# Attention masks turned by DMA transposes instead of TensorE and ScalarE, in a two-layer graph network kernel

## The chip, the cores and the metric

The kernel runs on one core of a Trainium2 chip. The metric is the device time of one execution in microseconds (us). The kernel before takes 4320.45 us, the median of three runs (4317.54 to 4321.28).

## The reference

For each of 16 batches there are 1024 nodes with 256 features (`x`) and an adjacency matrix of 1024 x 1024 int32 (`adj`, about 3% ones). Two layers follow each other, and both use the same adjacency as a mask:

```python
def heads(x):
    return x.reshape(w, n, H, DH).transpose(0, 2, 1, 3)          # 8 heads of 32
q, k, v = heads(features @ Wq), heads(features @ Wk), heads(features @ Wv)
e = jnp.einsum('whqd,whkd->whqk', q, k)
e = jnp.where(e >= 0, e, ALPHA * e)                              # leaky relu, 0.2
attn = jax.nn.softmax(jnp.where(adj[:, None] > 0, e, NEG), axis=-1)
h = jnp.einsum('whqk,whkd->whqd', attn, v)
out = _layernorm(h, g1, b1)
out = jnp.concatenate([out, features], axis=-1) @ Wffn.T
x = _layernorm(out, g2, b2) + features
# second layer: two graph attentions, then a feed-forward net
def _gat(h, adj, W, a, out_features):
    Wh = h @ W
    e = leaky_relu(Wh @ a[:F] + swap(Wh @ a[F:]))                # 1024 x 1024 by broadcast
    return softmax(where(adj > 0, e, NEG), axis=1) @ Wh
h = _layernorm(x + _gat(_gat(x, W1, a1), W2, a2))
out = _layernorm(h + relu(h @ w_ff1 + b_ff1) @ w_ff2 + b_ff2)
```

Inputs and outputs are float32.

## The kernel before, in words

`unshifted_path` does the work with softmaxes that subtract no maximum; `general_path` is a second program that runs only if a check of sums and scores at the end asks for it, which it does not for these inputs.

Per batch and head, scores are made with keys on the partitions and queries along the row: for each of 8 key tiles t, two matmuls of 128x512 (L615) make a 128x1024 tile in PSUM. ScalarE scales it by 0.2 (L631), VectorE takes the maximum with the original (L633), ScalarE takes the exponential (L636), GpSimd multiplies it with the mask (L640), and TensorE multiplies the result with the values and with a column of minus ones for the sums, 32 columns of weights at a time (L655, `product`). These value products are called narrow below. VectorE also adds two pairs of tiles per head first (L699). After a head, VectorE turns the result (L716) and GpSimd divides by the sums (L723). When all heads of a batch are done, `rest(b)` runs: `rows_pair` (L792, L795, L812, L824) closes layer one, `attention`/`attend` (L860 to L885) with the products L915 and L940 are the two graph attentions, `hidden` and `feed_forward` (L980, L1008) the feed-forward net. `rest(b)` runs while the heads of batch b + 1 run.

Because keys lie on the partitions, the mask is needed with rows and columns exchanged. `mask_part(b, t, halves)` makes it for 128 queries: it loads 128x512 int32 of the adjacency into a buffer of the pool `pair` (L424 by the SP queue for batch 0, L420 by the ACT queue afterwards, two halves in one part), VectorE turns it into bytes, -1 or 0 in fp8, in a buffer `adjb` (L429), TensorE transposes these as pairs of bytes, that is as 2-byte elements, four transposes of 128x128 per part of two halves, into a PSUM buffer of the pool `misc` (L439), and ScalarE copies the PSUM buffer to the mask (L443). `mask_of(b, t)` reads one tile of it with a stride of two bytes. A mask is 1024 bytes x 8 on each partition, and there are two, so the mask of batch b + 1 is made during batch b. The multiply L640 of batch b waits for the parts of all queries; the graph attentions read the same mask (L880).

The queries and keys of a batch are split into a high and a low float32 part and stored to DRAM (L504, SP's queue), and read back for each head as stacks (`qs`, `ks`, four loads on SP's queue, L581); there are two buffers of each. The first layer's result of a batch is stored and fetched again too (L754, L761), and the output stored (L1023), all on SP's queue.

The order of all instructions on every engine is written out by a planner, `Order`, when the program is built. The parts above are generators that say which engine they need for how long (`on(PE=310)`), which buffers they take and give, and for what they wait. Each has a due time, its aim, as a share of the batch's planned time SLOT; the tables AIM (batches from the third on) and EARLY (batch 0 and 1) hold these shares. Whichever operation can start within 300 ns of the earliest and has the smallest aim goes next. A DMA is `load(n)`: 500 ns of its queue for each n, and a landing some 3.5 us later. The engines and queues then run these orders as they are, each instruction waiting by semaphores for what it needs; DMAs of both queues share eight semaphores, and a DMA waits until the earlier one on its semaphore has landed.

Of the kernel before, what the change touches and what calls it, by code (L numbers as in the profile page):

```python
# [11 lines left out]
BF = mybir.dt.bfloat16  # L12
F8 = mybir.dt.float8e4
I32 = mybir.dt.int32
AF = mybir.ActivationFunctionType
OP = mybir.AluOpType
# [4 lines left out]
P = 128  # L21
HALF = 512
# [164 lines left out]
def on(shared=False, delay=0.0, mode=None, **costs):  # L187
    return "on", (costs, shared, delay, mode)


def pause(time):
    return "pause", time


def wait(event):
    return "wait", event


def fire(event):
    return "fire", event  # L200


def take(pool):
    return "take", pool


def give(pool):
    return "give", pool


def start(thread, aim):
    return "start", (thread, aim)
# [21 lines left out]
def unshifted_path(  # L234
# [8 lines left out]
    nc = tc.nc  # L243
    B, N, D = x.shape
    NT = N // P
    NP = NT // 2
# [8 lines left out]
    QN = N // 4  # L255
# [4 lines left out]
    YW = D + 2  # L260
    NSUM = NT * H + 2 * NT
    NSCORE = 4 * NT
    SLOT = 253e3
    PACE = SLOT / (H * NT // 2)


    AIM = dict(mask0=0.602, x=1.454, x_step=-0.0104, mask=0.9396, mask_step=-0.0101, qk0=0.4907, qk1=1.7441,
               qk_step=-0.0518, v0=0.7416, v1=0.621, v_step=0.0547, rows=-0.079, rows_step=-0.0113, first0=0.2137,
               first1=-0.446, graph0=-0.0793, graph1=0.316, graph_step=0.0481, second=0.7493, second_step=-0.015,
               normed=1.0223, normed_step=-0.0115, ff_wait=(None, 0, 1, 0), ff=(0.5532, 0.1074, 3.6996, 1.0353),  # L270
               ff_step=0.0063, fast0=0.2312, fast1=0.6979, fast15=1.0127, lead=14.8372)

    EARLY = dict(x=2.6481, x_step=-0.1001, mask=0.5019, mask_step=0.0795, qk0=0.7532, qk1=1.2626, qk_step=-0.1325,
                 v0=0.2134, v1=1.5023, v_step=-0.0416, rows=-2.7213, rows_step=-0.3343, first0=-0.8482,
                 first1=-4.695, graph0=0.0441, graph1=-0.9035, graph_step=-0.1073, second=0.463,
                 second_step=0.0554, normed=0.7744, normed_step=0.0342, ff_wait=(None, 0, 1, 0),
                 ff=(2.0875, 0.7055, 1.5112, 0.6358), ff_step=0.0607)

    const = ctx.enter_context(tc.tile_pool(name="const", bufs=1))
    sb = ctx.enter_context(tc.tile_pool(name="sb", bufs=1))  # L280
    small = ctx.enter_context(tc.tile_pool(name="small", bufs=6))
    psum = ctx.enter_context(tc.tile_pool(name="psum", bufs=2, space=bass.MemoryType.PSUM))
    dram = ctx.enter_context(tc.tile_pool(name="dram", bufs=3, space=bass.MemoryType.DRAM))
    bufs = dict(misc=3, scores=2, acc=1, p=6, stacks=2, stage=2, adj=2, adjb=2, pair=18,
                xT=2, v=2, mask=2, hn=1, w8=2, big=1, job=1)
    work = Order(**bufs)

    def share(b, name):
        return (EARLY if b < 2 else AIM)[name]

    def misc(dtype=FT):
        return psum.tile([P, HALF], dtype, tag=f"misc{work.slot['misc']}", name="ps_m", bufs=1)

    def buf(shape, tag, name, dtype=FT):
        return sb.tile(shape, dtype, tag=tag, name=name, bufs=bufs[tag])


    ident = const.tile([P, P], FT, name="ident")
    make_identity(nc, ident)
    ident_b = const.tile([P, P], BF, name="ident_b")  # L300
    nc.vector.tensor_copy(ident_b, ident)
    eps = const.tile([P, 1], FT, name="eps")
    nc.gpsimd.memset(eps, EPS)
    minus_ones = const.tile([P, DH], FT, name="minus_ones")
# [18 lines left out]
    k = {}  # L323
# [15 lines left out]
    def load(n=1, latency=3500):  # L339

        return on(SP=500 * n, delay=latency)
# [56 lines left out]
    masks = {}  # L398
# [3 lines left out]
    stacks = {}  # L402

    def mask_part(b, t, halves):

        n = len(halves)
        ints = []
        if b:
            yield take("adj")
        elif halves[0]:  # L410
            yield wait(("mask", b, t, 0))
        for kh in halves:
            yield take("pair")
            ai = buf([P, HALF], "pair", "adj_i", I32)
            ints.append(ai)
            part = adj[b].rearrange("(u p i) k -> u i p k", p=P, i=2)[t // 2, t % 2, :, kh * HALF:(kh + 1) * HALF]
            if b:
                yield pause(1500)
                yield on(ACT=400, delay=3500)
                nc.scalar.dma_start(ai, part)  # L420
            else:
                yield pause(2000)
                yield load()
                nc.sync.dma_start(ai, part)  # L424
        yield take("adjb")
        ab = buf([P, 2 * HALF], "adjb", "adj_b", F8)
        for i, ai in enumerate(ints):
            yield on(DVE=336, shared=True)
            nc.vector.tensor_scalar(ab[:, i * HALF:(i + 1) * HALF], ai, 0.0, -1.0,  # L429
                                    op0=OP.is_gt, op1=OP.mult, saturate=False)  # L430
            yield give("pair")
        if b:
            yield give("adj")
        yield take("misc")
        pt = misc(BF)
        pairs = ab.bitcast(BF)
        yield on(PE=30 + 140 * n)
        for i in range(2 * n):
            nc.tensor.transpose(pt[:, i * P:(i + 1) * P], pairs[:, i * P:(i + 1) * P], ident_b)  # L439
        yield give("adjb")  # L440
        yield on(ACT=46 + 218 * n)
        k0 = 2 * halves[0]
        nc.scalar.copy(masks[b].bitcast(BF).rearrange("p (k q) -> p k q", k=NP)[:, k0:k0 + 2 * n, t * P:(t + 1) * P],  # L443
                       pt[:, :2 * n * P].rearrange("p (k q) -> p k q", k=2 * n))
        yield give("misc")
        for kh in halves:
            yield fire(("mask", b, t, kh))

    def make_mask(b, t0):
        yield take("mask")  # L450
        masks[b] = buf([P, NT * N], "mask", "mask", F8)
        parts = [(t, (kh,)) for kh in range(NH) for t in range(NT)] if b == 0 else [(t, (0, 1)) for t in range(NT)]
        for n, (t, halves) in enumerate(parts):
            yield start(mask_part(b, t, halves),
                        t0 + ((share(b - 1, "mask") if b else AIM["mask0"]) + share(b - 1, "mask_step") * n) * SLOT)

# [54 lines left out]
    def project_qk(b, g, t0):  # L511
        scratch[b, g] = dram.tile([2, P, 2, N], FT, name="qk_halves")
        for o in range(2):
            for nh in range(NH):
                yield start(qk_part(b, g, o, nh), t0 + (2 * o + nh) * share(b - 1, "qk_step") * SLOT)

# [20 lines left out]
    def project_v(b, g, t0):  # L537
        yield take("v")
        vs[b, g] = buf([P, NT, G * DH], "v", "v")
        for u in range(NP):  # L540
            yield start(v_part(b, g, u), t0 + share(b - 1, "v_step") * u * SLOT)

# [6 lines left out]
    def project(b, t0):  # L549
        yield take("xT")  # L550
        xTs[b] = buf([P, DC, N], "xT", "xT")
        for u in range(NP):
            yield start(x_pair(b, u), t0 + (share(b - 1, "x") + share(b - 1, "x_step") * u if b else 0.0) * SLOT)
        yield start(make_mask(b, t0), t0 + (0.5 if b else 0.0) * SLOT)
        for g in range(H // G):
# [35 lines left out]
    def pace(b):  # L591
        return PACE * {0: AIM["fast0"], 1: AIM["fast1"], B - 1: AIM["fast15"]}.get(b, 1.0)

    def all_scores():
        for b in range(B):
# [4 lines left out]
            for h in range(H):  # L600
                yield wait(("stack", b, h))
                q, kk = stacks[b, h]
                for t in range(NT):
                    due = t0 + (h * NT + t) / 2 * pace(b)
                    if b == 0 or t % 2 == 0:
                        yield aim(due, AIM["lead"] * PACE)
                        for _ in range(2 if b else 1):
# [877 lines left out]
```

## Time and profile before

The profile is of one execution of the kernel before.

| | |
|---|---|
| median of three runs | 4320.45 us |
| the profiled execution | 4317.81 us |
| its span, first to last instruction | 4315.9 us |
| mean granted TensorE clock | 0.990 |
| L439, transposes of the mask, PE | 512, 219 ns median, 52.2 us busy |
| L443, copies of the mask, ACT | 136 (120 of 582 ns, 16 of 376 ns) |
| L429, conversions, DVE | 256, 761 ns mean, 421 ns median in a steady batch |
| L640, multiply with the mask, POOL | 1024, 2431 ns |
| DMA, both queues | 344.79 MB, 80 GB/s mean |

Times are in microseconds unless marked ns. PE is TensorE, PEld its weight loads, DVE VectorE, ACT ScalarE, POOL GpSimd, SP the sync engine that only issues DMAs; SPq and ACTq are the issue of DMAs. L439 is line 439 of the kernel. "busy" is the union of an engine's instructions; matmuls overlap, so a mean duration of one is longer than the time it holds the queue. A row of waits names the waiting instruction, then the one whose end released it, then total us, times and the longest. A line of the order of time begins with start and length in us.

### The profile page before, as it was taken

How to read it: one execution, taken by the hardware profiler on the slowest of the kernel's cores; microseconds unless marked ns; L12 is line 12 of the kernel's file. 1: busy time of each engine (PE TensorE's matmuls, PEld its weight loads, DVE VectorE, ACT ScalarE, POOL GpSimd, SP SyncE). 2: the span in 40 equal slices, each digit the busy share in tenths (PEclk: the TensorE clock that was granted, in tenths of full speed). 3: DMA queues.
4: the chain of work that ended last, by engine and by line, in shares of the span. 5: the costliest groups of instructions: out<-in, count | busy, mean ns of one | idle time of the engine just before them, and what ended most of it. 6: DMA issues, size and time to landing. Idle time of an engine off the chain costs nothing.

```text
span 4315.9 us, 76274 instructions
## 1 busy us (share of the span) xinstructions
PE 4189.7 (97%) x30027; PEld 3030.3 (70%) x30027; DVE 3544.8 (82%) x5491; ACT 2942.7 (68%) x4362; POOL 2571.6 (60%) x1161
## 2 busy tenths in 40 slices
PE   8788999999999999999999999999999999999999
PEld 4466677677777777777777777777777777777687
DVE  6878878888888887879879788887889879788853
ACT  6756677777767677776776767677776776767632
POOL 5846467664757656574664757646575674747700
PEclk9999999999999999999999999999999999999999
DMA  6413223322232322323232222322323222222100
GB/s 188 125 54 99 69 76 87 91 72 86 74 94 67 96 84 68 90 71 89 84 84 81 79 81 79 91 73 81 91 74 89 81 84 84 74 79 57 30 20 21
DMA packets 156282, 344.79 MB, mean 80 GB/s; under 512 B 21750, under 2 KB 24332, under 8 KB 155916
## 3 DMA queue, kind: packets, MB, share of 16 engines
q1 hardware_dynamic: 112140, 260.13, 21.0%
q10 hardware_dynamic: 43776, 79.71, 6.6%
q8 instruction: 239, 3.92, 0.4%
q14 instruction: 127, 1.04, 0.1%
HBM read 239.09 MB, written 100.66 MB: 79 GB/s over the span
## 4 chain that ended last, share of the span: by engine, by line
PE 82%; DVE 11%; ACT 3%; POOL 1%; DMA 1%; issue 1%; SPq 0%; ACTq 0%; POOLq 0%; DVEq 0%
PE ps_a L655 17%; PE ps_s L615 11%; PE ps_m L915 10%; PE ps_m L980 9%; PE ps_m L940 9%; PE ps_m L1008 7%; PE ps_m L492 4%; DVE p L633 3%; PE ps_m L792 3%; PE ps_m L824 3%; PE ps_m L795 3%; PE ps_m L524 2%; PE ps_m L372 2%; DVE p L699 2%; POOL p L640 1%; DVE att L880 1%
## 5 line engine op out<-in xcount | busy, mean ns | idle before, releaser
L640 POOL TENSOR_TENSOR p<-p,mask 128x1024 f32<-128x1024 f32 x1024 | 2471.1, 2431 | 1425.5 <-ACT p L636 1044.1
L633 DVE TENSOR_TENSOR p<-p,ps_s 128x1024 f32<-128x1024 f32 x1024 | 1211.3, 1213 | 251.2 <-ACT p L631 248.1
L636 ACT ACTIVATE p<-p 128x1024 f32<-128x1024 f32 x1024 | 1082.2, 1059 | 302.3 <-DVE p L633 276.7
L631 ACT ACTIVATE p<-ps_s 128x1024 f32<-128x1024 f32 x1006 | 986.3, 1021 | 345.2 <-PE ps_s L615 283.0
L615 PE MATMUL ps_s<-qs,ks 128*128 128x512 f32 x2048 | 658.7, 437 | 30.6 <-DVE p L633 27.0
L655 PE MATMUL ps_a<-p,v 128*32 128x256 f32 x8192 | 561.9, 388 | 24.4 <-POOL p L640 24.3
L615 PEld LDWEIGHTS ps_s<-qs,ks 128*128 128x128 f32 x2048 | 352.6, 190 | 266.1 <-issue 114.8
L940 PE MATMUL ps_m<-y,att 128*128 128x256 f32 x2048 | 481.1, 382 | 12.6 <-ACT y L885 11.1
L915 PE MATMUL ps_m<-y,att 128*128 128x258 f32 x2048 | 477.1, 383 | 14.4 <-ACT y L885 12.9
L980 PE MATMUL ps_m<-rT,wf 128*128 128x256 f32 x2048 | 474.3, 383 | 9.4 <-ACT hid L989 4.3
L1008 PE MATMUL ps_m<-wf,hid 128*128 128x256 f32 x2048 | 475.7, 381 | 0.6 <-DVE hid L986 0.6
L915 PEld LDWEIGHTS ps_m<-y,att 128*128 128x128 f32 x2048 | 385.5, 190 | 89.3 <-ACT y L885 13.8
L980 PEld LDWEIGHTS ps_m<-rT,wf 128*128 128x128 f32 x2048 | 381.0, 190 | 85.9 <-issue 14.3
L699 DVE TENSOR_TENSOR p<-p 128x1024 f32<-128x1024 f32 x256 | 410.5, 1604 | 23.6 <-PE ps_a L655 23.4
L940 PEld LDWEIGHTS ps_m<-y,att 128*128 128x128 f32 x2048 | 378.4, 190 | 71.1 <-ACT y L885 11.3
L1008 PEld LDWEIGHTS ps_m<-wf,hid 128*128 128x128 f32 x2048 | 379.1, 190 | 63.6 <-issue 8.2
L655 PEld LDWEIGHTS ps_a<-p,v 128*32 128x32 f32 x8192 | 209.5, 109 | 289.3 <-issue 130.8
L655 PE MATMUL ps_a<-p,minus_ones 128*32 128x256 f32 x6144 | 405.8, 382 | 1.2 <-DVE p L699 1.2
L877 DVE SCALAR_TENSOR_TENSOR att<-first,second 128x1024 f32<-128x1024 f32 x256 | 359.7, 1405 | 32.4 <-ACT first L864 28.3
L880 DVE SCALAR_TENSOR_TENSOR att<-mask,att 128x1024 f32<-128x1024 fp8e4 x256 | 339.5, 1326 | 5.6
L655 PEld LDWEIGHTS ps_a<-p,minus_ones 128*32 128x32 f32 x6144 | 199.1, 111 | 138.3 <-issue 7.9
L885 ACT ACTIVATE y<-y,check 128x258 f32<-128x258 f32 x256 | 131.1, 512 | 220.4 <-DVE check L883 217.9
(101 smaller groups left out, 4330.0 us busy)
## 6 DMA issues: line engine op xcount, KB each, us to landing
qs<-qk_halves SPq DMA_DIRECT2D x256, 256.0 KB, 4.0
ks<-qk_halves SPq DMA_DIRECT2D x256, 256.0 KB, 5.2
adj_i<-in_adj_dram ACTq DMA_DIRECT2D x240, 256.0 KB, 3.1
qk_halves<-high SPq DMA_DIRECT2D x128, 256.0 KB, 2.8
qk_halves<-low SPq DMA_DIRECT2D x128, 256.0 KB, 3.6
xr<-in_x_dram ACTq DMA_DIRECT2D x64, 256.0 KB, 4.7
x_kept<-x SPq DMA_DIRECT2D x64, 256.0 KB, 2.0
x<-x_kept SPq DMA_DIRECT2D x64, 256.0 KB, 5.1
```

What stands on the lines that cost most here:

```text
L615: nc.tensor.matmul(ps[:, cols], kk[:, t * P:(t + 1) * P], q[:, cols], start=True, stop=True)
L631: nc.scalar.activation(p, ps, AF.Copy, scale=ALPHA)
L633: nc.vector.tensor_tensor(p, p, ps, op=OP.max)
L636: nc.scalar.activation(p, p, AF.Exp)
L640: nc.gpsimd.tensor_tensor(p, p, mask_of(b, t), op=OP.mult)
L655: nc.tensor.matmul(acc[i * DH:(i + 1) * DH, at:at + QN].rearrange("d (t r) -> d t r", r=DH), w, p.rearrange("k (t i r) -> k i t r", i=4, r ...
L699: nc.vector.tensor_tensor(ps[to], ps[to], ps[by], op=OP.add)
L880: nc.vector.scalar_tensor_tensor(e, mask_of(b, j), -1.0, e, op0=OP.mult, op1=OP.mult, accum_out=sums[:, j:j + 1])
L915: nc.tensor.matmul(pa[:, cols:cols + width], big[:, j, i * P:(i + 1) * P], rows[:, j, :width], start=(j == 0), stop=(j == NT - 1))
L940: nc.tensor.matmul(pa[:, i * D:(i + 1) * D], big[:, j, t * P:(t + 1) * P], y2[:, j, :D], start=(j == 0), stop=False)
L980: nc.tensor.matmul(pa[:, i * 2 * P:(i + 1) * 2 * P], wf1[:, dc, hc * P:(hc + 1) * P], rT[:, dc, :], start=(dc == 0), stop=(dc == DC - 1))
L1008: nc.tensor.matmul(pa[:, i * D:(i + 1) * D], hid[hc // 2][:, hc % 2, i * P:(i + 1) * P], wf2[:, hc, :], start=(hc == 0), stop=False)
```

## The change

The buffer `adjb`, its pool and the 2-byte identity are gone. The conversion writes its bytes over the loaded words: the 512 results of a half (2048 bytes per partition) go to the first 256 bytes of each of its two kilobytes. In place of the transposes of TensorE and the copy of ScalarE, SP issues two DMA transposes of 128x128 2-byte elements for each half, from the buffer to the mask, and gives the buffer back when they have landed. The planner counts the two as one load. The pool `pair` has 19 buffers for 18. SLOT is 250e3 for 253e3, and all aims are new, so every engine's order differs from before. Lines below the change move up by 2 to 10.

```diff
--- before.py
+++ after.py
@@ -260,28 +260,28 @@
     YW = D + 2
     NSUM = NT * H + 2 * NT
     NSCORE = 4 * NT
-    SLOT = 253e3
+    SLOT = 250e3
     PACE = SLOT / (H * NT // 2)
 
 
-    AIM = dict(mask0=0.602, x=1.454, x_step=-0.0104, mask=0.9396, mask_step=-0.0101, qk0=0.4907, qk1=1.7441,
-               qk_step=-0.0518, v0=0.7416, v1=0.621, v_step=0.0547, rows=-0.079, rows_step=-0.0113, first0=0.2137,
-               first1=-0.446, graph0=-0.0793, graph1=0.316, graph_step=0.0481, second=0.7493, second_step=-0.015,
-               normed=1.0223, normed_step=-0.0115, ff_wait=(None, 0, 1, 0), ff=(0.5532, 0.1074, 3.6996, 1.0353),
-               ff_step=0.0063, fast0=0.2312, fast1=0.6979, fast15=1.0127, lead=14.8372)
-
-    EARLY = dict(x=2.6481, x_step=-0.1001, mask=0.5019, mask_step=0.0795, qk0=0.7532, qk1=1.2626, qk_step=-0.1325,
-                 v0=0.2134, v1=1.5023, v_step=-0.0416, rows=-2.7213, rows_step=-0.3343, first0=-0.8482,
-                 first1=-4.695, graph0=0.0441, graph1=-0.9035, graph_step=-0.1073, second=0.463,
-                 second_step=0.0554, normed=0.7744, normed_step=0.0342, ff_wait=(None, 0, 1, 0),
-                 ff=(2.0875, 0.7055, 1.5112, 0.6358), ff_step=0.0607)
+    AIM = dict(mask0=-0.6814, x=3.1353, x_step=-0.0764, mask=0.815, mask_step=0.0319, qk0=0.8106, qk1=3.0541,
+               qk_step=0.1879, v0=1.1019, v1=0.433, v_step=0.1526, rows=-0.2236, rows_step=-0.0644, first0=0.3079,
+               first1=-0.3892, graph0=0.1118, graph1=0.4386, graph_step=-0.1677, second=2.115, second_step=-0.1703,
+               normed=2.343, normed_step=-0.1446, ff_wait=(None, 0, 1, 0), ff=(1.2864, 0.3301, 3.1909, 2.1168),
+               ff_step=0.1935, fast0=0.1034, fast1=0.7089, fast15=1.4986, lead=20.4511)
+
+    EARLY = dict(x=2.5086, x_step=-0.175, mask=0.1855, mask_step=0.114, qk0=0.714, qk1=1.419, qk_step=-0.2214,
+                 v0=0.6646, v1=3.1702, v_step=0.1953, rows=-1.5958, rows_step=-0.1751, first0=-1.0232,
+                 first1=-4.7447, graph0=-0.2592, graph1=0.0497, graph_step=0.0447, second=0.518,
+                 second_step=-0.0255, normed=0.7025, normed_step=0.0523, ff_wait=(None, 0, 1, 0),
+                 ff=(3.8018, 1.1685, 2.0265, 0.5888), ff_step=0.1724)
 
     const = ctx.enter_context(tc.tile_pool(name="const", bufs=1))
     sb = ctx.enter_context(tc.tile_pool(name="sb", bufs=1))
     small = ctx.enter_context(tc.tile_pool(name="small", bufs=6))
     psum = ctx.enter_context(tc.tile_pool(name="psum", bufs=2, space=bass.MemoryType.PSUM))
     dram = ctx.enter_context(tc.tile_pool(name="dram", bufs=3, space=bass.MemoryType.DRAM))
-    bufs = dict(misc=3, scores=2, acc=1, p=6, stacks=2, stage=2, adj=2, adjb=2, pair=18,
+    bufs = dict(misc=3, scores=2, acc=1, p=6, stacks=2, stage=2, adj=2, pair=19,
                 xT=2, v=2, mask=2, hn=1, w8=2, big=1, job=1)
     work = Order(**bufs)
 
@@ -297,8 +297,6 @@
 
     ident = const.tile([P, P], FT, name="ident")
     make_identity(nc, ident)
-    ident_b = const.tile([P, P], BF, name="ident_b")
-    nc.vector.tensor_copy(ident_b, ident)
     eps = const.tile([P, 1], FT, name="eps")
     nc.gpsimd.memset(eps, EPS)
     minus_ones = const.tile([P, DH], FT, name="minus_ones")
@@ -422,27 +420,19 @@
                 yield pause(2000)
                 yield load()
                 nc.sync.dma_start(ai, part)
-        yield take("adjb")
-        ab = buf([P, 2 * HALF], "adjb", "adj_b", F8)
-        for i, ai in enumerate(ints):
+        for ai in ints:
             yield on(DVE=336, shared=True)
-            nc.vector.tensor_scalar(ab[:, i * HALF:(i + 1) * HALF], ai, 0.0, -1.0,
-                                    op0=OP.is_gt, op1=OP.mult, saturate=False)
-            yield give("pair")
+            nc.vector.tensor_scalar(ai.bitcast(F8).rearrange("p (s k) -> p s k", s=2)[:, :, :QN],
+                                    ai.rearrange("p (s k) -> p s k", s=2), 0.0, -1.0, op0=OP.is_gt, op1=OP.mult,
+                                    saturate=False)
         if b:
             yield give("adj")
-        yield take("misc")
-        pt = misc(BF)
-        pairs = ab.bitcast(BF)
-        yield on(PE=30 + 140 * n)
-        for i in range(2 * n):
-            nc.tensor.transpose(pt[:, i * P:(i + 1) * P], pairs[:, i * P:(i + 1) * P], ident_b)
-        yield give("adjb")
-        yield on(ACT=46 + 218 * n)
-        k0 = 2 * halves[0]
-        nc.scalar.copy(masks[b].bitcast(BF).rearrange("p (k q) -> p k q", k=NP)[:, k0:k0 + 2 * n, t * P:(t + 1) * P],
-                       pt[:, :2 * n * P].rearrange("p (k q) -> p k q", k=2 * n))
-        yield give("misc")
+        for kh, ai in zip(halves, ints):
+            yield load()
+            for i in range(2):
+                nc.sync.dma_start_transpose(masks[b].bitcast(BF).rearrange("p (k q) -> p k q", k=NP)
+                                            [:, 2 * kh + i, t * P:(t + 1) * P], ai.bitcast(BF)[:, i * HALF:i * HALF + P])
+            yield give("pair")
         for kh in halves:
             yield fire(("mask", b, t, kh))
```

## The prediction

> **What bounds the kernel now.** I read the page's first two parts, then the table of windows, then the waits, then the order of time around one mask part. First, who is full:
>
> ```profile
> span 4315.9 us, 76274 instructions
> PE 4189.7 (97%) x30027; PEld 3030.3 (70%) x30027; DVE 3544.8 (82%) x5491; ACT 2942.7 (68%) x4362; POOL 2571.6 (60%) x1161
> ...
> PE   8788999999999999999999999999999999999999
> ```
>
> TensorE is busy 97% of the span; nothing else comes near. The windows (start:end, then busy time of PE, PEld, DVE, ACT, POOL with instruction counts, granted clock, DMA share, GB/s) say where the other 3% lies:
>
> ```profile
> 0.00:100.00 100.00, 79.01 (x495) 42.00 (x496) 65.05 (x74) 62.29 (x86) 56.32 (x34) 0.91 0.63 189
> 100.00:360.00 260.00, 218.56 (x1738) 135.65 (x1737) 204.69 (x268) 173.86 (x240) 177.53 (x83) 0.93 0.34 96
> 360.00:620.00 260.00, 240.09 (x1731) 172.34 (x1731) 213.04 (x334) 173.95 (x252) 149.97 (x70) 0.96 0.28 78
> ...
> 1400.00:1660.00 260.00, 258.24 (x1876) 187.96 (x1872) 221.55 (x344) 183.97 (x271) 161.15 (x73) 1.00 0.29 82
> ```
>
> From about 880 us on, every batch is alike: in the chain that ended last, the same piece of L915 stands at 1351.81 and at 1611.96, so a batch takes 260.15 us, and PE is busy 258.2 of 260 at full clock. DVE has 38 us to spare per batch, ACT 76, POOL 99, the DMA engines 71%. The idle PE time is mostly early: 21 + 41.4 + 19.9 + 5.4 us in the four windows up to 880. So in steady state a microsecond taken from PE is a microsecond of the batch, if nothing else then comes late.
>
> Next, what the mask work costs PE, and who waits for it (order of time on PE, then the lines for who waited for whom: total us, times, longest):
>
> ```profile
> 1501.06 0.38 PE L439 MATMUL ps_m<-ident_b,adj_b 128*128 128x128 bf16 x4
> 1501.38 1.12 PE L655 MATMUL ps_a<-p,v 128*32 128x256 f32 x16
> ...
> 1503.29 0.40 PE L439 MATMUL ps_m<-ident_b,adj_b 128*128 128x128 bf16 x4
> 1503.52 1.95 PE L940 MATMUL ps_m<-y,att 128*128 128x256 f32 x8
> ```
>
> ```profile
> POOL p L640 <- ACT mask L443: 306.1, 15, 27.3
> ...
> PE ps_a L655 <- POOL p L640: 24.3, 31, 2.1
> ...
> PEld ps_m L792 <- ACT mask L443: 6.3, 11, 0.6
> ```
>
> A group of four transposes holds the queue from its start to the start of the next group: 0.32 and 0.23 us here. The row's mean of 219 ns for one is latency, overlapped with its neighbours.
>
> **The change part by part.** *PE transposes removed.* I took that start-to-start time for all groups of L439 in the trace, less idle: 37.1 us in all, 0.279 us for a part of four in steady state. Of the 512 transposes 30 lie before the first scores (39 us), where PE waits for loads anyway; 482/512 of 37.1 leaves **-34.9 us** on the path.
>
> *ACT copies removed.* 136 copies of 586 ns (376 for the halves) are 75.3 us of ACT, 1.7% of the span; ACT has room, so this alone is nothing. But L792 waits for the PSUM buffer that the copy empties: 3.7 us of PE idle over the run. **-3.7 us.**
>
> *DVE conversions.* Still 256, 421 ns median, now written over the words just read, in two runs of 256 bytes. I take the same time; if the split output cost it its speed, the nearest dearer row is L497 (680 ns for as many elements): 0.26 us x 16 = 4 us of DVE per batch, inside its 38 us. Nothing.
>
> *512 DMA transposes added, all on SP's queue.* The trace has none. Two costs: SP's issue time X, and the landing L. Below, X is no less than SP's cheapest row, 0.32 us. Above, the Trainium skill prices the operation: "VectorE: DVE Perf Modes", section "The three transpose paths", gives 390 ns for a 128x128 2-byte transpose on TensorE against 1309 ns by DMA, and its rules send it to TensorE if PSUM will do. That speaks against this change. But the row says that TensorE's price here is 0.279/4 = 0.07 us of queue, not 0.39, and that it is paid on the full engine, while a DMA's price falls on queues that are idle most of the time. If each 1.31 us lay on the path, 482 of them would cost 630 us against 35 saved; on SP's queue 32 per batch are 42 us beside some 29 us of present issues in 260 (32 of 0.58, 16 of 0.33, 12 of 0.4). I take X = 0.6, SP's dearest row (qs and ks, 0.55 to 0.6 each), and L = 2.8 (the median of stores from SBUF in this trace), between 2.0 and 5.2. Bytes: 512 x 32 KB = 17 MB on 345; nothing.
>
> *What is late at a batch's start.* POOL's first multiply of a batch waits for all mask parts. In the trace the last conversion ends at 1522.5, its transposes start at 1525.5, its copy ends at 1526.8, and POOL starts:
>
> ```profile
> 1526.90 8.51 POOL L640 TENSOR_TENSOR p<-p,mask 128x1024 f32<-128x1024 f32 x4 [21.77 <-ACT mask L443]
> ```
>
> That is 4.4 us after the conversion. In the new instruction order the last conversion stands behind the fifth max of head 0, in the old behind the fourth: alike. After it come four transposes on SP and the landing: 4 x 0.6 + 2.8 = 5.2 us. The planner counts two issues of 0.5 and some 3.65 to land, 4.65, so PE's new order allows for that much; 0.55 beyond it, in 15 batches, is **+8 us** (0 if they land as planned). POOL has 38% free, but PE stands behind POOL in order (L655 waits, above), so lateness passes on. Conversions of parts are 4 to 8 us apart (1501.7, 1509.7, 1513.7, 1521.8), so SP falls behind only if 4X exceeds 6.7 us.
>
> *Behind a transpose on SP* wait stack loads (qs, ks), q/k stores, and the x1 traffic. In steady state 6, 2, 8 and 16 transposes stand between stack loads some 25 to 35 us apart; each stack has a second buffer, so 16 x 0.6 = 10 us is covered, and 16 x 1.31 = 21 still is. Each DMA also waits for an earlier one's semaphore, of eight shared with ACT's loads; ACT lost 19.3 us to such waits (L631 after adj_i). With 1.3 times as many DMAs, perhaps 10 more, inside ACT's 32%. Pair buffers are held until the transposes land; there are 19 for 18. Nothing for either.
>
> *The start.* Here the queue matters (SP's issues: start, length):
>
> ```profile
> 16.69 0.33 SPq L504 DMA_DIRECT2D qk_halves<-high  x1
> ...
> 23.32 4.30 SPq L424 DMA_DIRECT2D adj_i<-in_adj_dram  x6
> 27.85 1.15 SPq L581 DMA_DIRECT2D qs<-qk_halves  x2
> 29.05 1.42 SPq L581 DMA_DIRECT2D ks<-qk_halves  x2
> ```
>
> The first scores need the load issued at 27.85. In the new order 22 transposes stand before it. Eight fit where SP is now idle, 9.3 to 16.7 (4.8 of 7.4 us). The other 14 cost 8.4 us, of which 3.9 fill gaps between 16.69 and 27.85: **+4.5 us** (0 at X = 0.32; 3 + 18.3 - 3.9 = 17.5 at 1.31). It passes whole to the end, as PE has little else yet.
>
> *Re-planning.* The new PE order has 508 runs of value products for 530; entering and leaving one costs about 0.29 us by the intervals between starts; 22 fewer could give 6. I take **-4**. SLOT (253 to 250 thousand) is a target and adds no work. The new aims for the first batches may win or lose part of the 67 us idle from 100 to 880; I take 0, bounds -25 to +25.
>
> **Sum**: -34.9 - 3.7 + 8 + 4.5 - 4 = -30.1. The profiled execution took 4317.8 us (span 4315.9), giving 4287.7; the median of the runs, 4320.45, is 2.6 above it: **4290 us**.
>
> **Rivals.** *A, slower: masks land late.* If X is 1.31 and L is 5.2, the last part needs 10.4 us instead of 4.4; 6 us per batch outweigh the 2.5 saved (0.279 x 8 plus the wait for the copy), so 3.5 x 14 and the long start (17.5) give about 4387 at the full price, 4350 at half. It decides from 4X + L above 6.9 us, that is, X over 1.0 with L at 2.8. For it: the skill's price, POOL's 21.77 us wait in each batch, PE's order behind POOL. Against: SP's rows are all under 0.6. *B, no change:* about 4320, if start and lateness together eat 34 us: X about 0.9. *C, more gain:* the early idle shrinks by 25 and masks land as planned: about 4260. For it: 67 us of early idle at lower clock; against: nothing in the old trace shows what the new aims do.
>
> **How the numbers follow.** Forecast 0.50 (4272 to 4308), A 0.30, B 0.10, C 0.10. A measurement of this kernel tells a change from none at about 0.2%, 8.6 us. Faster: forecast and C, 0.60; same: B, 0.10; slower: A, 0.30. The range leaves out half of C below (4262) and half of A above (4375).
>
> **What would show it.** Right: a period near 257.7 between like pieces in the chain, PE still busy 99% of a steady window, L439 and L443 gone, SP's transposes at 0.6 each, POOL's wait at a batch's start no more than a few us longer and L655 waiting for POOL under 1 us per batch, the first qs issue near 32 us. Wrong: a PE busy share of 96% or less in steady windows with L655 behind POOL and POOL behind a DMA on the mask (A); transposes of over 1 us on SP; ACT waiting long at its adj_i issues, a wait that I costed at nothing.

## The result: slower by 2.6%

| | before | after |
|---|---|---|
| median, us | 4318.99 (4313.07 to 4321.28, 4 runs) | 4429.02 (4426.17 to 4432.9, 4 runs) |
| ratio, 95% interval | 1 | 1.0258 (1.024 to 1.0275) |
| span of the profiled execution, us | 4315.9 | 4427.1 |
| start of the first scores, us | 39.1 | 56.5 |
| batch 0, from its first scores to those of batch 1 | 168.9 | 184.6 |
| batches 1, 2, 3, 4 | 260.8, 258.7, 251.2, 258.5 | 259.0, 264.7, 262.3, 269.0 |
| mean of batches 5 to 14 | 260.2 | 264.6 |
| from the first scores of batch 15 to the end | 477.0 | 484.9 |

The kernel before has one run more here than ahead of the prediction, hence its other median. The lower rows are the start of every 128th matmul of L615 (L605 in the changed kernel). The loss of 111 us is 17.4 at the start, 15.7 in batch 0, 25.8 in batches 1 to 4, 4.4 in each of ten steady batches, and 8 at the end.

The page of the changed kernel, first its busy times, then the rows of 40 slices and of packets:

```profile
span 4427.1 us, 76398 instructions
PE 4183.5 (94%) x29515; PEld 3033.1 (69%) x29515; DVE 3594.9 (81%) x5513; ACT 2863.9 (65%) x4203; POOL 2519.7 (57%) x1161
...
PE   5788999998999999999999999999999999999998
...
PEclk7989999999999999999999999999999999999999
...
DMA packets 238208, 361.65 MB, mean 82 GB/s; under 512 B 103670, under 2 KB 106252, under 8 KB 237836
```

The 512 transposes are gone from TensorE (29515 matmuls for 30027), yet its busy time fell by only 6 us. The DMA packets rose from 156282 to 238208, but the loads that the scores wait for are not slower by it: the stacks `qs` and `ks` land 4.1 and 5.0 us (medians) after their issue, before 4.0 and 5.2. The windows (start:end, busy time of PE, PEld, DVE, ACT, POOL, granted clock, DMA share, GB/s):

```profile
0.00:100.00 100.00, 53.98 (x277) 29.89 (x278) 38.30 (x47) 33.55 (x43) 28.01 (x22) 0.76 0.60 166
...
1400.00:1660.00 260.00, 252.53 (x1797) 184.63 (x1799) 218.13 (x336) 174.61 (x257) 153.57 (x71) 0.99 0.30 84
1560.00:1620.00 60.00, 54.78 (x362) 42.81 (x352) 46.82 (x107) 35.39 (x72) 19.62 (x11) 0.94 0.34 95
...
1595.00:1600.00 5.00, 4.25 (x10) 3.44 (x11) 3.21 (x10) 0.50 (x2) 2.08 (x1) 0.50 0.14 52
```

In a steady window TensorE idles 7.5 us for 1.8 before, most of it in one stretch after a batch's first scores (here at 1560.4). By the trace's clock records its clock is granted at half from 1594.5 us, near the end of that idle stretch, for 6.8 us. Over the whole trace such half-clock stretches add up to 206.5 us (31 stretches), before to 90.4 us (14).

The rows of waits on PE (total, times, longest) name two new ones:

```profile
PE ps_m L782 <- DVE y L326: 51.5, 11, 4.7
...
PE ps_s L605 <- DMA ks<-qk_halves: 21.3, 1, 21.3
```

The second is the start. SP's order of time there:

```profile
10.19 10.12 SPq L433 DMA_TRANSPOSE mask<-adj_i  x8
...
25.07 8.51 SPq L433 DMA_TRANSPOSE mask<-adj_i  x6
...
49.12 1.23 SPq L571 DMA_DIRECT2D qs<-qk_halves  x2
50.40 1.24 SPq L571 DMA_DIRECT2D ks<-qk_halves  x2
52.16 12.59 SPq L433 DMA_TRANSPOSE mask<-adj_i  x10
```

A transpose holds SP for 1.22 us. The first stacks are issued at 49.1 instead of 27.85 us, and ten more transposes stand before the second.

The first wait comes once in every steady batch. The order of time there, on POOL, DVE and PE:

```profile
1584.32 12.76 POOL L630 TENSOR_TENSOR p<-p,mask 128x1024 f32<-128x1024 f32 x6 [15.13 <-DMA mask<-adj_i]
```

```profile
1581.43 0.75 DVE L425 TENSOR_SCALAR adj_i<-adj_i 128x512 fp8e4<-128x512 int32 x2
...
1585.21 3.53 DVE L364 TENSOR_SCALAR y<-y,mv,rs 128x256 f32<-128x256 f32 x2 [0.93 <-ACT rs L355]
...
1591.75 3.35 DVE L364 TENSOR_SCALAR y<-y,mv,rs 128x256 f32<-128x256 f32 x2
1595.02 0.68 DVE L326 COPY y<-ps_m 128x512 f32<-128x512 f32 x1
```

```profile
1595.76 2.08 PE L782 MATMUL ps_m<-wffnT,xT 128*128 128x256 f32 x4 [4.69 <-DVE y L326]
```

GpSimd's first multiply of the batch comes 23.9 us after the first scores, where it came at 29.5 before: the masks are early, not late. Its burst of six then lies over two pairs of VectorE's normalisations L364, which take 3.53 and 3.35 us instead of 0.73. The copy L326 stands behind them and frees the PSUM buffer that L782 needs, so TensorE waits 4.7 us and then runs at half clock: four matmuls of L782 take 2.08 us, where four take 1.06 at 1586.5.

In the kernel before, the pair nearest to the burst began 1.3 us ahead of GpSimd's first multiply (1526.90) and was through in time:

```profile
1525.65 0.74 DVE L366 TENSOR_SCALAR y<-y,mv,rs 128x256 f32<-128x256 f32 x2 [0.23 <-ACT rs L357]
```

Of the 5.6 us by which the multiply is earlier, 3.3 come from the new order, which ends the last conversion 21.8 us after the first scores (25.1 before), and 2.3 from the shorter way from there to the mask.

Over the whole trace: of the 384 instructions of L364, the 308 that began outside a GpSimd multiply took at most 0.42 us; of the 76 that began inside one, 57 took over 1 us, up to 2.23, about the length of one multiply (2.1 to 2.2). The statistics L348 took 0.40 us in both cases. The DMA transposes are not what slows L364: the kernel before has none, and there too 30 of the 66 that began inside a multiply took over 1 us, and none of the 318 outside over 0.42. This agrees with what the Trainium skill, "SBUF — State Buffer", section "SBUF: two separate sides", says of a port pair that VectorE and GpSimd share: for some kinds of VectorE instruction it is an exclusive lock for a whole instruction, on which the later one blocks. Which of the kinds that the page lists L364 is, no run here tests.

### The profile page after: what moved, and what is told of

Same layout as the page of the kernel before. It is cut to its first block, busy times and chain, and to the rows that moved or that the text cites. A ratio compares the mean times of both kernels' runs of the same rounds, so it can differ in the third digit from the quotient of the medians.

```text
span 4427.1 us, 76398 instructions
## 1 busy us (share of the span) xinstructions
PE 4183.5 (94%) x29515; PEld 3033.1 (69%) x29515; DVE 3594.9 (81%) x5513; ACT 2863.9 (65%) x4203; POOL 2519.7 (57%) x1161
## 2 busy tenths in 40 slices
DMA packets 238208, 361.65 MB, mean 82 GB/s; under 512 B 103670, under 2 KB 106252, under 8 KB 237836
## 4 chain that ended last, share of the span: by engine, by line
PE 73%; DVE 18%; ACT 4%; issue 2%; POOL 1%; DMA 1%; SPq 1%; ACTq 0%; DVEq 0%; POOLq 0%
PE ps_a L645 16%; PE ps_s L605 10%; PE ps_m L930 10%; PE ps_m L905 10%; PE ps_m L970 7%; PE ps_m L998 6%; DVE att L867 4%; DVE att L870 4%; PE ps_m L482 3%; DVE p L623 3%; PE ps_m L814 2%; PE ps_m L782 2%; PE ps_m L785 2%; DVE y L364 2%; PE ps_m L370 2%
## 5 line engine op out<-in xcount | busy, mean ns | idle before, releaser
L630 POOL TENSOR_TENSOR p<-p,mask 128x1024 f32<-128x1024 f32 x1024 | 2438.4, 2400 | 1308.8 <-ACT p L626 657.7
L605 PE MATMUL ps_s<-qs,ks 128*128 128x512 f32 x2048 | 648.8, 434 | 67.1 <-DVE p L623 45.5
L605 PEld LDWEIGHTS ps_s<-qs,ks 128*128 128x128 f32 x2048 | 353.2, 191 | 287.7 <-issue 79.3
L689 DVE TENSOR_TENSOR p<-p 128x1024 f32<-128x1024 f32 x256 | 442.1, 1727 | 31.2 <-PE ps_a L645 30.4
L870 DVE SCALAR_TENSOR_TENSOR att<-mask,att 128x1024 f32<-128x1024 fp8e4 x256 | 329.5, 1287 | 7.4
L713 POOL TENSOR_TENSOR hn<-ho,check 128x256 f32<-128x256 f32 x128 | 87.5, 684 | 386.4 <-DVE check L711 362.6
```

What stands on the lines that cost most here:

```text
L605: nc.tensor.matmul(ps[:, cols], kk[:, t * P:(t + 1) * P], q[:, cols], start=True, stop=True)
L630: nc.gpsimd.tensor_tensor(p, p, mask_of(b, t), op=OP.mult)
L870: nc.vector.scalar_tensor_tensor(e, mask_of(b, j), -1.0, e, op0=OP.mult, op1=OP.mult, accum_out=sums[:, j:j + 1])
```

## The experiments

Three theories. **E (early)**: the transposes land earlier than the written order allows for; GpSimd's burst meets VectorE's normalisations, TensorE waits and loses clock; the start's queue on SP is a second, separate loss. **Q (queue)**: 1.22 us per issue makes masks or stacks late in every batch. **P (order)**: the new aims are slower in themselves. Each ratio below is to the kernel before as timed together with that run (medians of 4312.9 to 4316.4 us).

**No transposes, constant masks.** All adjacency ones in effect; the conversions remain.

```diff
-                nc.sync.dma_start_transpose(masks[b]...)
+                pass
-        masks[b] = buf([P, NT * N], "mask", "mask", F8)
+        masks[b] = fixed[b % 2]
```

> The changed kernel with its order kept, but with no DMA transposes: both masks are constant tiles of -1, written once at the start, so every node attends to all others and the output is not the reference's. Loads and conversions of the adjacency stay. Theories: E (early): the transposes land some 6.5 us sooner after the conversion than the planner counted, so GpSimd's first six multiplies of a batch run into VectorE's normalisations (L364)[...], and TensorE then waits 4.7 us at L782 and loses its clock for a while. Q (queue): at 1.22 us of SP each, transposes make masks and stacks late. P (plan): the new order is slower by itself. P expects the steady batch to stay at 264 to 265 us and the first scores at 56 us, total above 4410. Q expects first scores near 40 us, batch 0 near 170, a steady batch at or under 259 us, total near 4330. E expects the start as Q does; the steady batch anywhere from 257 to 264, since multiplies that never wait meet other VectorE work.

Measured: 4353.02 us, ratio 1.009 (1.007 to 1.011). First scores at 43.8 us, batch 0 176.7, steady batches 260.4. GpSimd, waiting for no mask, multiplies one to three tiles at a time; the wait of L782 for L326 is gone. By the ratios the mechanism costs some 72 us in this order, but the order without it is still not as fast as the kernel before, although TensorE has no transposes at all here: P has a share. By the profile 29 us of the loss against the kernel before lie ahead of batch 5. Some 4 of these are the edit's own: GpSimd first writes the constant masks (6.9 us for one of 128x8192 bytes), and TensorE begins at 8.2 us instead of 4.4 in the changed kernel. The same holds for the other kernels with constant masks below.

**No transposes in batch 0 alone** (that batch's weights are not masked).

```diff
+                if b:
                     nc.sync.dma_start_transpose(masks[b]...)
```

> Only batch 0 has no DMA transposes (its mask is set to -1 once, so batch 0's output is not the reference's); order kept. If transposes on SP's queue delay the start (both E and Q): first scores near 40 us in place of 56.5, batch 0 near 170 us in place of 184.6, total down by some 30 us to near 4398, the steady batch unchanged at 264.5. If the late start is the new order's (P): first scores stay at 56 us and the total within 5 us of 4429.

Measured: 4407.42 us, ratio 1.0216 (1.0196 to 1.0237). SP's order of time at the start:

```profile
31.30 1.15 SPq L575 DMA_DIRECT2D qs<-qk_halves  x2
32.50 2.54 SPq L575 DMA_DIRECT2D ks<-qk_halves  x2
```

First scores at 42.3, batch 0 176.3, all later batches as in the changed kernel. The start's queue is worth 22 us by the medians, 18 by the ratios; but for the writing of the constant mask it might be some 4 more.

**Each part's transposes in reverse order.** The work is the same; what GpSimd needs first is issued last of its part's four.

```diff
-        for kh, ai in zip(halves, ints):
+        for kh, ai in reversed(list(zip(halves, ints))):
             yield load()
-            for i in range(2):
+            for i in (1, 0):
```

> The four transposes of a part are issued in the reverse order (second half first, second byte group first), so the one that the first multiply of a batch waits for is issued last; order of all engines kept, nothing left out. The first multiply then starts some 6 us later after the first scores, near the 30 us that the planner counted, in place of 23.9. E expects the wait of L782 for L326 to shrink from 4.7 us to under 1.5, the steady batch from 264.5 to between 257.5 and 260.5 us, total 4350 to 4385. Q expects the reverse: masks later still, the steady batch 267 us or more, total above 4460. P expects no change, within 10 us of 4429.

Measured: 4358.52 us, ratio 1.0098 (1.0081 to 1.0114): 70 us faster than the changed kernel by delaying the masks. GpSimd starts at 30.6 to 31.8 us after the first scores, and two pairs of L364 have gone before it. VectorE and GpSimd in the batch that starts at 1548.0:

```profile
1572.84 0.73 DVE L364 TENSOR_SCALAR y<-y,mv,rs 128x256 f32<-128x256 f32 x2 [0.93 <-ACT rs L355]
...
1576.96 0.73 DVE L364 TENSOR_SCALAR y<-y,mv,rs 128x256 f32<-128x256 f32 x2
1577.82 0.69 DVE L326 COPY y<-ps_m 128x512 f32<-128x512 f32 x1
...
1580.40 3.23 DVE L364 TENSOR_SCALAR y<-y,mv,rs 128x256 f32<-128x256 f32 x2
```

```profile
1579.21 12.87 POOL L630 TENSOR_TENSOR p<-p,mask 128x1024 f32<-128x1024 f32 x6 [22.39 <-DMA mask<-adj_i]
```

The third pair is still blocked, but the wait of L782 for L326 is gone, and TensorE idles 2.5 to 4.4 us in a steady batch for 7.0 in the changed kernel. Steady batches take 259.4 us, under the 260.2 of the kernel before, and half-clock stretches fall to 148.2 us. E, and against Q: later masks are better here.

**Transposes of 64 rows for 128** (half of each mask; the rest constant).

```diff
-                                            [:, 2 * kh + i, t * P:(t + 1) * P], ai.bitcast(BF)[:, i * HALF:i * HALF + P])
+                                            [:, 2 * kh + i, t * P:t * P + P // 2],
+                                            ai[:P // 2].bitcast(BF)[:, i * HALF:i * HALF + P])
```

> Each DMA transpose moves 64 rows in place of 128 (the other half of each mask stays at the constant -1, so the output is not the reference's); order kept. It asks what the issue time of 1.22 us goes by. If by the amount: about 0.6 to 0.7 us each, first scores near 47 us, total down by 15 to 35 us. If it is fixed per instruction: 1.1 to 1.2 us each, first scores within 3 us of 56.5, total within 12 us of 4429. E expects no gain in the steady batch beyond 1.5 us, Q expects 2 us or more per batch if the issue time falls.

Measured: 4435.0 us, ratio 1.028 (1.0259 to 1.0301), as the changed kernel. The rows of SP's transposes (shortest/median/longest in ns), full size first:

```profile
L433 SPq DMA_TRANSPOSE mask<-adj_i x512: 1093/1224/2502, 10.2 to 3969.9; - x171
```

```profile
L436 SPq DMA_TRANSPOSE fixed<-adj_i x512: 1088/1219/2809, 15.5 to 3972.9; - x171
```

Half the bytes, the same issue time, and the same 2.8 us to land: between 64 and 128 rows the price is per instruction. First scores came at 60.8 us, later than I had allowed for a fixed price (53.5 to 59.5); the writing of the constant masks accounts for some 4 us.

**Reversed, and none in batch 0.** Both edits above.

> The changed kernel with both earlier edits at once: every part's transposes issued in reverse order, and none at all for batch 0 (whose mask is a constant -1, so that batch's weights aren't masked). Theory E with the start as a separate cost: the two gains add, 4358.5 - (4429.0 - 4407.4) = 4337 us, between 4330 and 4346, with first scores near 42 us, batch 0 near 176-180 us and steady batches near 259.4. What is left over the kernel before (about 20 us) would then be the new order of the work by itself. If the early collision and the start's queue were one loss counted twice, the time stays at 4350-4360. If the order were not slower by itself, it would fall to 4320 or below.

Measured: 4332.46 us, ratio 1.0049 (1.0032 to 1.0066). The gains add. What is left over the kernel before is 21 us by the ratio. By the profile the start and the first batches lose about as much (first scores at 43.1, then 174.4, 256.5, 260.9, 259.3, 264.3), while steady ones, at 258.9, gain. In its first 480 us TensorE waits 35.9 us for VectorE's maxima, before 17.5, one of these waits 12.6 us long; the kernel without transposes has that wait of 12.6 us too, so it belongs to the order, as P says. The 21 us are a remainder, not the order's price: the saving of TensorE's transposes is already taken off, and what the transposes of batches 1 to 4 cost is in it.

**Only the two halves exchanged.**

```diff
-        for kh, ai in zip(halves, ints):
+        for kh, ai in reversed(list(zip(halves, ints))):
```

> The changed kernel with only the two halves of a part exchanged: the transposes of the second half are issued first, the two of each half in their old order, so the first ones that GpSimd needs go out two issues, 2.45 us, later instead of four less one, 3.7 us. Theory E (the masks come so early that GpSimd's burst meets VectorE's two pairs of normalisations): GpSimd's first multiply of a steady batch moves from 23.9 to about 26.4 us after the first scores, the first pair (at 24.8 us) runs free in 0.7 us and the second, which follows sooner, may or may not be met; the wait of L782 for L326 falls from 4.7 to 0-2.5 us, the steady period to 259.4-262.5, the total to 4358-4405. Theory P (the order itself): no change, 4425-4433. Theory Q (masks too late): slower by 2.45 us in each batch, about 4465.

Measured: 4359.28 us, ratio 1.0107 (1.0091 to 1.0124), steady batches 260.0. GpSimd starts at 29.3 to 30.7, not 26.4: six transposes of two parts stand in a row in SP's queue there, the pair that GpSimd needs is now the last of them instead of the first, and so it goes out four issues later. My figure for the start was missed; the time is inside E's range and the effect is nearly that of full reversal. The first pair runs clear in every steady batch; the last of the second pair's two instructions still meets the burst in six of ten (2.3 us for 0.41), and TensorE's wait at L782 is down to 9.3 us in the whole run, from 51.5.

These runs leave open whether the mechanism could pay at all. The next ones keep the order of the kernel before (its aims, its `adjb`, the planner's steps) and exchange the mechanism only.

**Old order, batches 1 to 15 by DMA.**

```diff
+        if b == 0:
...
+        else:
+            for i in range(2 * n):
+                nc.sync.dma_start_transpose(masks[b]...[:, k0 + i, t * P:(t + 1) * P], pairs[:, i * P:(i + 1) * P])
```

> The kernel before with its own aims and order of work kept, and the mechanism alone exchanged in batches 1 to 15: the parts' transposes go out on SyncE's queue where ACT copied the mask, first half first; batch 0 stays on TensorE. If the transposes by DMA themselves pay (theory E: what was lost lay in the start and in the order made for a wrong cost), TensorE gets back 0.279 us x 8 in each of 15 batches and the 3.7 us of waits for the copy: 4313 - 33 - 4 = 4276, between 4270 and 4295, with a steady period near 257.8; the upper end holds if GpSimd's burst, some 2 us earlier than in the kernel before, meets VectorE's normalisations. Theory Q (SyncE's queue or late masks make the mechanism slow): 4313 or more, with TensorE behind GpSimd (L655). If the time is equal within 5 us, TensorE's transposes had been free.

Measured: 4356.11 us, ratio 1.0093 (1.0077 to 1.011). My expectation failed: slower. But the steady batches aren't alike. In order, from batch 5: 263.1, 258.1, 263.5, 257.5, 261.0, 263.8, 261.5, 261.1, 261.0, 264.3, with TensorE idle for 4.6, 1.2, 5.1, 1.2, 3.7, 5.1, 3.7, 4.5, 3.5, 5.4 us. Two of them have the gain that was forecast: there the pair of normalisations nearest to GpSimd's start begins 1.0 to 1.1 us ahead of it, and each instruction takes 0.41 us. In the other eight the pair begins within 0.3 us after GpSimd's first multiply, and its instructions take 2.0 to 2.3 us. Batches 1 to 4 lose 22 us (267.0, 263.3, 257.6, 263.7): there some parts are converted 2 to 4 us apart, less than their four issues of 1.22 us, and SP falls behind; conversions then wait for their buffer `adjb` (23.5 us in 20 waits on these transposes in the whole run, 12.2 of them in four waits up to 1262 us), and GpSimd starts 4.9 us later in batch 4. So Q holds in the early batches, where parts are close together.

**The same with the second half first.** The one edit is `for i in (2, 3, 0, 1)`.

> As the kernel before with the transposes by DMA in batches 1 to 15 under the old order, but with the second half's transposes first, so that the masks which GpSimd needs first come 2.5 to 6 us later. Where a later mask is what helped in the changed order because of the collision alone, it doesn't help here: GpSimd starts at about 32 to 35 us after a batch's first scores for 29.5 in the kernel before, and TensorE waits for its multiplies; slower than with the first half first by 5 to 40 us, 4285-4315. If later masks are better in any order, it is faster.

Measured: 4343.59 us, ratio 1.005 (1.0032 to 1.0067), so faster than with the first half first, against my expectation. Steady batches are better (259.5 on the mean, GpSimd at 29.9 to 31.2), early ones worse (175.2 for batch 0, then 268.6, 271.7, 259.9, 264.4), with TensorE waiting 11.5 us for POOL between 360 and 1140 us, where it waited 0.8 before. Later is better where the masks are early, and worse where they are late already.

**Old order, batch 0 by DMA too.** As in the kernel with batches 1 to 15 by DMA, first half first, but with no branch for batch 0.

> As the kernel before with the transposes by DMA under the old order, first half first, and now in batch 0 too. Theory E with the start as a cost of its own: the first stack loads stand behind the transposes on SyncE's queue at 1.22 us each; first scores move from 39 to 50-58 us, and the total is 15 to 25 us above the one with batch 0 on TensorE. If the start's loss came with the new order, the difference is under 5 us.

Measured: 4369.39 us, ratio 1.0122 (1.0105 to 1.0139), 13 us above the one with batch 0 on TensorE by the medians. First scores at 58.7 us and batch 0 182.3 in the profiled run, which took 17 us longer than the other three, so its start may be worse than theirs. The start's loss is the mechanism's own, not the new order's; its size was a little over-stated.

**Old order, batches 5 to 15 by DMA, the transpose that is needed first issued as the second of four.**

```diff
+        turned = b >= 5
...
+        if turned:
+            for i in (2, 0, 3, 1):
+                nc.sync.dma_start_transpose(masks[b]...[:, k0 + i, t * P:(t + 1) * P], pairs[:, i * P:(i + 1) * P])
```

> The kernel before with its own order of work; batches 0 to 4 stay on TensorE, batches 5 to 15 are turned by DMA, with the transpose that GpSimd needs first issued as the second of its part's four. Under the old order the batches in which GpSimd's burst began clear of VectorE's normalisations ran in 257.5 to 258.3 us for 260.15, those where it met them in 260 to 264. Theory E (what TensorE is spared is gained whole where nothing collides): GpSimd starts at 28.5 to 30 us after the first scores, 10 batches save 1.5 to 2.3 us each, the start and the early batches are as before, and the total is 15 to 25 us under the kernel before: 4291-4301. If the burst still meets the normalisations in most batches (offsets under 28.5): 4310-4330. If TensorE's transposes are free in fact: 4316, the same.

**The same batches, but two of a batch's eight parts stay on TensorE** (`turned = b >= 5 and t < 6`, in plain order).

> As the kernel before with batches 5 to 15 turned by DMA under the old order, but only six of a batch's eight parts; the last two, which decide when GpSimd may start, stay on TensorE and ACT. Theory E: GpSimd's first multiply stays at 29.5 us, no collision, and TensorE is spared 6 x 0.279 = 1.7 us in each of 11 batches: 16 to 22 us under the kernel before, 4294-4301, with steady periods of 258.2-258.8, all alike. If the gain needs the last parts too, or the queue on SyncE delays something else, the period stays at 260 and the total at 4310-4320.

Measured, the first: 4289.34 us (4287.09 to 4292.95, 5 runs), ratio 0.9942 (0.9928 to 0.9955), faster than both kernels, and 24 us under the kernel before by the medians, inside the 15 to 25 that E expected. The second: 4321.55 us, ratio 1.002 (1.0013 to 1.0026), no gain. My assumption that GpSimd would stay at 29.5 us was wrong, for the edit doesn't do what I meant: `mask_step` is negative, so the parts with t of 6 and 7 are not the last in time. In the trace ACT's two copies come 3.8 and 6.1 us after the first scores, and the part that is converted last, at 23.2, goes by DMA. What the second kernel shows is a batch whose last part is issued in plain order, so that GpSimd starts earlier than in the first, at 26.1 to 26.7 for 27.5 to 29.6. The pair shows the lock plainly. The first kernel, batch at 1746.3:

```profile
1773.74 0.73 DVE L366 TENSOR_SCALAR y<-y,mv,rs 128x256 f32<-128x256 f32 x2 [0.23 <-ACT rs L357]
```

```profile
1775.01 8.50 POOL L646 TENSOR_TENSOR p<-p,mask 128x1024 f32<-128x1024 f32 x4 [19.86 <-DMA mask<-adj_b]
```

The second kernel, batch at 1752.2:

```profile
1778.68 4.12 DVE L366 TENSOR_SCALAR y<-y,mv,rs 128x256 f32<-128x256 f32 x2 [0.23 <-ACT rs L357]
```

```profile
1778.38 8.49 POOL L646 TENSOR_TENSOR p<-p,mask 128x1024 f32<-128x1024 f32 x4 [18.65 <-DMA mask<-adj_b]
```

Where VectorE's pair is ahead of GpSimd by 1.3 us it takes 0.73 us; where GpSimd is ahead by 0.3 us it takes 4.12. Steady batches: 258.3 us on the mean in the first, 260.9 in the second; two parts' transposes on TensorE are some 0.6 us of that difference, by the prediction's 0.279 each. And the first kernel's page:

```profile
span 4287.6 us, 76099 instructions
...
PE 4167.5 (97%) x29675; PEld 3008.5 (70%) x29675; DVE 3537.4 (83%) x5491; ACT 2891.8 (67%) x4274; POOL 2568.4 (60%) x1161
```

Of the 28 us that its span is shorter, 19 are the ten batches from 5 to 14, 2.4 the end; the other 6.8 lie ahead of batch 5's scores. Of these 1.5 are in batch 4, in which the first mask by DMA is made, and 5.5 in the start and batch 0, which the edit doesn't touch; so 21 to 23 us are the edit's.

## Why the prediction was wrong, by its steps

- **TensorE's transposes (-34.9) and waits for the copy (-3.7)** were sized about right. 2.5 us per batch were forecast; the two batches of the old order that had no collision ran in 257.5 and 258.1 for 260.2, and ten batches of the fastest kernel gave 1.9 each. In the changed kernel the saving can't be read off TensorE's busy time, which fell by 6 us: the half-clock stretches are 116 us longer, and matmuls take twice as long in them.
- **X = 0.6, L = 2.8.** L was right (median 2.8). X is 1.22, twice the value. I chose the dearest row of SP's present DMAs, which was not near: another kind of DMA has another price. The figure of the Trainium skill for a transpose by DMA ("VectorE: DVE Perf Modes", section "The three transpose paths"), which I kept as an upper end, was 1.31 and nearer; the page doesn't say whether it is issue or landing, and here the issue took 1.22 and the landing 2.8. The run with half-sized transposes adds that the price on SP is per instruction, for 64 rows as for 128.
- **"What is late at a batch's start" (+8)** failed in its sign, and this is the largest term. I let GpSimd's multiply wait for four transposes after the last conversion. It needs only the first of them for its first tile: the last conversion ends 21.8 us after the first scores, the multiply starts at 23.9, 2.1 us later, where the old way took 4.4. And I called the place of the last conversion in the two orders alike, while the new one ends it 3.3 us sooner after the scores. Together the multiply comes 5.6 us sooner. I had bounded the cost below by 0, as if early were free. A steady batch became 4.4 us longer, for GpSimd then holds what VectorE needs. The runs with reversed or exchanged transposes take that back: 69 us by the ratios.
- **The start (+4.5)** was the step with the right mechanism and a size that hung on X. The end of its range that I worked out for X = 1.31, 17.5, is what the first scores show (17.4), in part by luck: with the measured X of 1.22 the same sum gives 15.5. The second stacks stood behind ten more transposes, which I didn't count and which lengthen batch 0. Leaving batch 0's transposes out gave 18 to 22 us.
- **Re-planning (-4) and new aims (0, within 25).** Their sign was wrong, but their size isn't settled. With no transposes at all the new order is 39 us slower than the kernel before (some 4 of them the edit's own). With all masks by DMA, the old order (which keeps `adjb`) took 4369 us and the new one 4429. With the collision and batch 0's transposes taken out, 21 us remain. So what the order costs depends on what it is combined with, and may lie beyond the bound of 25. Why these aims are slower in the first batches no run shows.
- **DVE conversions at nothing** was right: L425 takes 760 ns on the mean for 761.
- **Rival A** said that masks landing late would give 4350 to 4387 and that it decides from X over 1.0. X was over 1.0 and the sign was A's, but not for its reason: in the steady batches masks came early. Its late masks are real only where parts are converted faster than SP issues, as in the early batches under the old order.

The loss taken apart step by step, by the runs' ratios: reversing the transposes gives back 69 us, leaving out batch 0's another 21, and 21 remain to the kernel before, together the 111 us that were lost. The first two are measured; the last is what is left, the order's cost and the early batches' queue less the saving. Taken in another sequence the shares would differ. Not tried: the new order with the transposes back on TensorE, which would have shown the order's cost alone; and a kernel without the clash that leaves GpSimd's burst where it is, for instance with the normalisations on another engine.

## What to carry to other kernels

When a change makes an input ready earlier, look at what its consumer then runs beside: here VectorE's 0.4 us instructions on SBUF took up to 2.2 us under GpSimd's multiplies, and within one run (old order, batches 1 to 15 by DMA) which of two starts came first, within about 1 us, went with 3 to 7 us of a batch. Count a DMA by its instructions on the queue that issues it (1.22 us each for these transposes, of 64 rows or of 128), and ask what stands behind them where the queue is dense, above all at the start. An order planned for one set of costs should be tried with the new mechanism alone before it is planned anew: kept for the steady batches only, the same mechanism was worth 0.6%.

## What the runs showed of the hardware

- A DMA transpose of 2-byte elements, SBUF to SBUF, holds SP's queue for 1.22 us at 128x128 and at 64x128, and lands 2.8 us (median) after its issue, at the least 2.2.
- A VectorE instruction from SBUF to SBUF that begins during a GpSimd multiply can wait for that multiply's end: L364 0.40 us outside, 1.5 on the mean inside, and the conversions L425 0.42 and 1.5; instructions that read PSUM (L387, 0.53 and 0.54) and the statistics (0.40 in both) don't.
- Within a stall of 4.7 us on TensorE (from 1591.1 us in the changed kernel) a stretch of 6.8 us at clock 0.50 began, at 1594.5, in which four matmuls of L782 took 2.08 us for 1.06; so it cost more than its length.
